# One causal-mask and row-maximum scheme, two routing strands and shared weight memory in a two-layer attention and expert kernel

## Chip, cores and metric

The kernel runs on one core of a Trainium2 chip. The metric is the device time of one execution in microseconds (us), and the figure for a kernel is the median of its runs. A profile is one more execution, recorded by the hardware; it has a time of its own.

A core has five instruction streams: PE (matrix products; the profile shows its weight loads apart, as PEld), DVE (vector work and row reductions), ACT (activations, exponentials), POOL (general work, and the indirect DMAs here) and SP (issues DMAs). Each engine takes its instructions in the order in which they were built. PE's results land in PSUM, which has eight banks of 128 partitions by 512 fp32 columns; DVE and ACT read them from there.

## The reference

`x` is [2, 2048, 256] in fp32. Cut to what matters:

```python
xn = layernorm(x)
s  = linear_attention(xn)        # rope, elu(q)+1, elu(k)+1, sum_k k v, / denominator, @ W_out
g  = silu(block(xn))             # see below
x  = x + s * g

xn = layernorm(x)
s  = attention(xn)               # Wq, Wk, Wv: 16 heads of 2*16 columns, causal softmax, Wo
g  = silu(xn @ int4_grid(kernel) + bias + (xn @ a) @ b)
x  = x + s * g

def block(x):                    # 16 heads of 16
    q, k, v = rope(ln1(x) @ Wqkv)
    x = x + causal_softmax(q k^T / 4) v @ Wproj
    flat = ln2(x)                                    # 4096 tokens
    gates = softmax(flat @ Wgate);  top 2 of 8 experts
    place = running count of the expert's tokens;  kept if place < 1024
    y_e = gelu(slots_e @ W1[e] + b1[e]) @ W2[e] + b2[e]
    return x + sum over the two experts of gate * y_e[place]
```

## The kernel before

`x` stays in SBUF as `xr`, 32 tiles of 128 tokens. Three stages follow one another.

**Layer-0 attention, with the linear attention beside it.** There are 8 groups of 4 heads (2 batches × 4). In a group, queries and keys lie turned in `qt` and `kt`, [128, 2048] each, one head in each 32 rows, so that four heads' products run in the four row groups of PE. A *unit* of the loop in `run_attention` (L514) holds two passes.

- Pass A (`pass_a`, L528): for 128 queries (tile t) and up to 512 keys (block k), each of 4 heads computes scores on PE into a bank of its own (L536), and DVE takes the largest of each row. Where the block holds the diagonal (k == t // 4) DVE does this with `tensor_tensor_reduce` (L543), which adds the causal constants of `causal`, a [128, 512] slice of the constants, and leaves the maximum; elsewhere with `tensor_reduce` (L547). The maxima are subtracted from the queries afterwards (`subtract`).
- Pass B (`pass_b`, L555 on): the same scores transposed (L562). Where they hold the diagonal, `hide` (L500) adds the mask on PE, by four bf16 products of an identity and a mask, each in 32 rows (L505). ACT takes exponentials out of the banks (L574). Later products with v (L804 in layer 0, L1557 in layer 1) sum over keys.

In a unit, the heads run in two halves, i = 0 and 2: pass A for heads i and i+1, pass B for the other two, in the order A(i), B(i+2), A(i+1), B(i+3), then pass B's masks, then the exponentials. There are 40 units in a group, with 640 pairs of heads in pass A in each layer: 256 of these pairs hold the diagonal.

Beside them run the preparation of the next group (`normalise0`, `norm`, `project`: normalise, turn, project, rotate on POOL, turn into qt and kt), the linear attention (`lin_keys`, `lin_out`, ending in stores of `lo` to `s_dram`, L1166), and at the end of each group of tiles the residual (L866), the second layernorm (statistics at L476 and L478 on DVE and small POOL operations), the logits (L930) and the picks: maxima, running counts, places and ways back (L940 to L987, some 35 small DVE operations). Tokens go to their slots by indirect DMAs from POOL (L1000).

**Experts.** For 2 halves × 8 experts: SP loads W1 (L1319), W2 (L1321), b2 (L1323) and the tokens `xe` (L1326); PE turns the tokens (L1335), multiplies by W1 (L1341) and W2 (L1347); results are stored (L1352). W1 and W2 each have two buffers of the pool that opens after the attention's pool has closed. The first `xe` waits for all sends. The constants of layer 1 are loaded behind it.

**Layer-1 attention**, same two passes with 32-wide heads; it starts with the normalised tiles `hn` (L1442), turned tiles `xt`, loads of `wg` (L1458), projections (L1468, L1483), and the gathers of expert results (L1403) for the mix of the later tiles.

In both attention stages a planner decides the order. Each piece of work is a step with a strand (its kind: S the products of both passes, A the maxima, B the exponentials, prep, sub, V, end, lin, moe, send, mix, gate, pair), an engine, a cost, and what it reads and writes. Steps of one strand on one engine keep their order; between strands the planner searches (a beam over short stretches) for the order that does most work, and gives out memory, the eight PSUM banks (kind "s") among it. The order found is then emitted, engine by engine. `others` in both stages lists parts with the unit at which they become due.

Names that come up below: `cst` the constants, `ident_h` and `mask_h` identity and mask for `hide`, `vt` the values with ones beside them (filled by DVE at L658), `lt` the low-rank gate's input, `carried` new memory.

## Time and profile before

| | us |
|---|---|
| median of 3 runs (lowest, highest) | 3483.42 (3477.35, 3490.22) |
| the profiled execution, its own time | 3508.01 |
| its span | 3506.2 |
| mean granted PE clock in it | 0.97 |
| busy PE / weight loads / DVE / ACT / POOL | 3350.0 / 2373.5 / 2163.6 / 1682.6 / 1660.5 |

Stages of that execution, by the marks in its timeline:

| stretch (us) | what runs |
|---|---|
| 0 to 32 | loads, constants, first tiles up to the first product of pass A at 31.59 |
| 32 to 1430 | layer-0 attention, linear attention beside it |
| 1430 to 1505 | last residuals, layernorm, logits, picks, sends; the linear attention's last tiles; first expert loads |
| 1505 to 1985 | experts |
| 1985 to 2050 | first projections of layer 1, gathers |
| 2050 to 3506 | layer-1 attention |

Other groups of the profile that are used below, in the form line, operation, count, mean:

| line | engine | what | count | mean ns |
|---|---|---|---|---|
| L562 | PE | pass B products, 256 or 128 columns | 9216 | 388 |
| L574 | ACT | exponential | 2304 | 576 |
| L804 | PE | values, layer 0 | 4608 | 381 |
| L1341 | PE | first expert product, 512 columns | 512 | 600 |

How to read it. A line of a group gives line, engine, operation, output and inputs with the tile's name, partitions by elements, the count, the busy time and the mean of one instruction; behind the bar stands the idle time of the engine just before, and what ended it. A line of the timeline gives the start, the duration, the engine (SPq is SP's queue of DMA issues), the line, the operation, a count where equal ones follow one another, and in brackets the idle time before it and its releaser. Matmul durations overlap, since four row groups work at once, so a mean of 559 ns does not mean that one ends each 559 ns.

### The profile page before, as it was taken

How to read it: one execution, taken by the hardware profiler on the slowest of the kernel's cores; microseconds unless marked ns; L12 is line 12 of the kernel's file. 1: busy time of each engine (PE TensorE's matmuls, PEld its weight loads, DVE VectorE, ACT ScalarE, POOL GpSimd, SP SyncE). 2: the span in 40 equal slices, each digit the busy share in tenths (PEclk: the TensorE clock that was granted, in tenths of full speed). 3: DMA queues.
4: the chain of work that ended last, by engine and by line, in shares of the span. 5: the costliest groups of instructions: out<-in, count | busy, mean ns of one | idle time of the engine just before them, and what ended most of it. 6: DMA issues, size and time to landing. Idle time of an engine off the chain costs nothing.

```text
span 3506.2 us, 81341 instructions
## 1 busy us (share of the span) xinstructions
PE 3350.0 (96%) x33814; PEld 2373.5 (68%) x33814; DVE 2163.6 (62%) x5599; ACT 1682.6 (48%) x3336; POOL 1660.5 (47%) x2223
## 2 busy tenths in 40 slices
PE   6999999999999999689989999999999999999998
PEld 4767777776777776456666556666776767777775
DVE  4777777777777877421121266667766657666774
ACT  3565555554555554311111265555445554554554
POOL 4443222323332221400000167989876657877877
PEclk7999999999999999789999999999999999999999
DMA  5000000000000000143333221010001010000000
GB/s 181 2 2 2 8 8 8 20 16 26 10 10 5 14 14 12 38 156 113 114 100 113 76 67 45 23 51 29 24 11 36 14 42 17 15 17 21 11 26 25
DMA packets 99508, 133.24 MB, mean 38 GB/s; under 512 B 9395, under 2 KB 76671, under 8 KB 99138
## 3 DMA queue, kind: packets, MB, share of 16 engines
q1 hardware_dynamic: 92994, 114.14, 10.1%
q0 software_dynamic: 6144, 13.88, 1.3%
q8 instruction: 266, 4.36, 0.5%
q14 instruction: 104, 0.85, 0.1%
HBM read 93.15 MB, written 37.75 MB: 37 GB/s over the span
## 4 chain that ended last, share of the span: by engine, by line
PE 45%; POOL 7%; DVE 2%; ACT 1%; issue 1%; DMA 1%; POOLq 0%; ACTq 0%; DVEq 0%
PE s L562 7%; PE s L536 7%; PE s L1347 6%; PE s L1341 6%; PE s L1557 6%; PE s L1468 3%; PE s L1526 2%; POOL ps L1542 2%; PE s L1563 2%; POOL ps L1543 2%; PE s L1605 2%; PE s L1483 1%; POOL ps L1538 1%; PE s L505 1%; PE s L1642 1%
## 5 line engine op out<-in xcount | busy, mean ns | idle before, releaser
L574 ACT ACTIVATE pt<-s 128x512 f32<-128x512 f32 (+1 forms) x2304 | 1168.9, 576 | 713.6 <-PE s L562 249.0
L562 PE MATMUL s<-qt,kt 32*128 32x256 f32 (+1 forms) x9216 | 1292.6, 388 | 7.9 <-ACT pt L574 4.4
L536 PE MATMUL s<-kt,qt 32*128 32x512 f32 (+3 forms) x5120 | 1269.7, 559 | 10.2 <-ACT pt L574 2.3
L547 DVE TENSOR_REDUCE mx<-s 128x1 f32<-128x512 f32 x1536 | 961.5, 682 | 185.0 <-PE s L536 101.9
L562 PEld LDWEIGHTS s<-qt,kt 32*128 32x128 f32 x9216 | 984.6, 185 | 62.0 <-ACT pt L574 16.2
L536 PEld LDWEIGHTS s<-kt,qt 32*128 32x128 f32 x5120 | 530.0, 186 | 170.0 <-issue 94.2
L543 DVE CUSTOM_DVE_ANT_0 s<-s,cst 128x128 f32<-128x128 f32 (+3 forms) x1024 | 482.3, 513 | 120.0 <-PE s L536 82.9
L1538 POOL TENSOR_TENSOR ps<-pt 128x1024 f32<-128x1024 f32 (+1 forms) x160 | 344.5, 2153 | 144.7 <-ACT pt L574 118.5
L743 POOL TENSOR_TENSOR ra<-raw,rope 128x128 f32<-128x128 f32 x128 | 58.6, 458 | 671.0 <-ACT raw L755 604.7
L1542 POOL TENSOR_TENSOR ps<-ps,pt 128x1024 f32<-128x1024 f32 x128 | 303.7, 2373 | 85.9 <-ACT pt L574 80.8
L1526 PE MATMUL s<-mh,ones_h 3*128 3x512 bf16 (+1 forms) x1152 | 317.3, 367 | 0.7 <-ACT mh L1519 0.7
L804 PE MATMUL s<-pt,vt 128*32 128x256 f32 (+1 forms) x4608 | 280.7, 381 | 5.3 <-issue 4.6
L1543 POOL TENSOR_TENSOR ps<-ps,pt 128x1024 f32<-128x1024 f32 (+1 forms) x128 | 269.2, 2103 | 10.0
L1557 PE MATMUL s<-pt,vt 128*32 128x256 f32 (+1 forms) x4608 | 271.3, 374 | 0.5 <-ACT pt L574 0.3
L1350 DVE TENSOR_TENSOR ye<-s,b 128x256 f32<-128x256 f32 x64 | 27.2, 424 | 391.6 <-PE s L1347 391.6
L1342 ACT ACTIVATE hm<-s,b1c 128x512 f32<-128x512 f32 x128 | 87.9, 687 | 359.6 <-PE s L1341 359.6
L1347 PE MATMUL s<-w,hm 128*128 128x256 f32 x1024 | 226.4, 382 | 8.5 <-ACT hm L1342 8.5
L1341 PE MATMUL s<-xt,w 128*128 128x512 f32 x512 | 226.4, 600 | 8.3 <-DVE xt L1282 8.3
L804 PEld LDWEIGHTS s<-pt,vt 128*32 128x32 f32 x4608 | 136.7, 112 | 135.0 <-issue 31.7
L1557 PEld LDWEIGHTS s<-pt,vt 128*32 128x32 f32 x4608 | 134.3, 110 | 136.4 <-DVE mx L547 18.0
L1347 PEld LDWEIGHTS s<-w,hm 128*128 128x128 f32 x1024 | 196.2, 192 | 42.9 <-ACT hm L1342 8.9
L505 PE MATMUL s<-mask_h,ident_h 32*128 32x256 bf16 x2048 | 197.7, 270 | 1.6 <-issue 1.6
(267 smaller groups left out, 4086.0 us busy)
## 6 DMA issues: line engine op xcount, KB each, us to landing
w<-in_L_ffn_W_dram SPq DMA_DIRECT2D x32, 1024.0 KB, 6.2
gl<-g_dram SPq DMA_DIRECT2D x64, 256.0 KB, 3.0
slots_in<-zero SPq DMA_DIRECT2D x8, 1024.0 KB, 10.2
xe<-slots_in SPq DMA_DIRECT2D x16, 512.0 KB, 8.0
slots_out<-ye SPq DMA_DIRECT2D x16, 512.0 KB, 7.2
xr<-in_L_attn_x_dram SPq DMA_DIRECT2D x4, 1024.0 KB, 5.6
s_dram<-lo SPq DMA_DIRECT2D x16, 256.0 KB, 2.0
hn<-in_L_attn_x_dram SPq DMA_DIRECT2D x16, 256.0 KB, 2.7
```

The lines of the kernel that those rows point to most:

```text
L536: nc.tensor.matmul(s.t[:, :w], g.qt.t[r, t * P : (t + 1) * P], g.kt.t[r, 512 * k : 512 * k + w], start=True, stop=True)
L543: nc.vector.tensor_tensor_reduce(s.t[:, :w], s.t[:, :w], causal[:, 512 - w :], 1.0, -3e38, ALU.add, ALU.max, to)
L547: nc.vector.tensor_reduce(to, s.t[:, :w], AX.X, ALU.max)
L562: nc.tensor.matmul(s.t[:, at], g.kt.t[r, kj * P : (kj + 1) * P], g.qt.t[r, QC * c + q0 : QC * (c + 1)], start=n == 0, stop=n == 1 and not ...
L574: S("B", "ACT", t_act(w), lambda: nc.scalar.activation(pt.t[:, j, :w], s.t[:, :w], AF.Exp, scale=0.25), r=[s], w=[(pt, j)])
L804: nc.tensor.matmul(av.t[32 * j : 32 * j + 32, q0:QC], vts[G.vn][:, kj, j], pt.t[:, j, at], start=n == 0, stop=n == len(tiles) - 1,)
L1341: nc.tensor.matmul(ps, w1[:, k, f * P : (f + 1) * P], xt[:, k], start=k == 0, stop=k == 1)
L1347: nc.tensor.matmul(ps[:, :D], hm[:, f, s * P : (s + 1) * P], w2[:, f], start=f == 0, stop=f == FF // P - 1)
L1526: return lambda: nc.tensor.matmul(s.t[:, :w_], ones_h[r], G.mh[c].t[r, 512 - w_ :], start=False, stop=last)
L1538: nc.gpsimd.tensor_tensor(ps.t[:, :, q0:], pt.t[:, :, same], pt.t[:, :, odd], ALU.add)
L1542: nc.gpsimd.tensor_tensor(ps.t, ps.t, pt.t[:, :, even], ALU.add)
L1557: nc.tensor.matmul(av.t[32 * j : 32 * j + 32, q0:QC], G.vt.t[:, kj, j], pt.t[:, j, at], start=n == 0, stop=False)
```

## The change

Seven edits, in one diff.

1. *Bank pairs.* PSUM's eight banks become one tile, and a buffer may ask for an even and an odd bank together. Pass A of two heads writes the two halves of a pair, and one `tensor_reduce` over [128, 2, w] gives both maxima.
2. *Mask on PE in layer 0's pass A.* On the diagonal, `hide` now adds the mask `mask_q` to the last 128 columns of each head's scores, after both heads' products and before pass B's own masks: 2 × 4 bf16 products of 32 rows and 128 columns for a pair. Layer 1 keeps `tensor_tensor_reduce`, one for each head, with its causal tile in memory of its own; the constants shrink from 1052 to 668 columns. A third set of `rep` copies and products at the start makes `mask_q`.
3. *Two strands for the routes.* What was "moe" is split: "moe" keeps statistics, scaling, turning and logits, "pick" has the picks.
4. *Carried memory.* Four tiles [128, 2048] are kept for the whole kernel. They serve as the two `qt` and the two `kt` of both layers, and, in between, as the two buffers of W1 and the two of W2.
5. *Layer 1's first tiles.* `hn`, `wg` and `xt` of layer 1 move to the pool that is open while the experts run; there is one `lt` in place of two.
6. *Start.* Tokens are loaded in pieces of 2, 2, 12 and 16 tiles (before: 4 × 8); the first four tiles are normalised in two parts of two; the fills of `vt` move from DVE to POOL and cover the ones' half alone; the turning into qt and kt, which followed each second `project`, becomes `turned_round` and is emitted one round later.
7. *Due times.* Batch 1's linear parts: from unit 172 on, one in each 9, where it was 180 and 7.5.

Counted in the built streams of all instructions, before and after: PE 22478 and 26578, DVE 5601 and 4068, ACT 3338 and 3338, POOL 2230 and 2249.

```diff
-    def __init__(self, kind):
-        self.kind, self.n, self.uses, self.t = kind, None, 0, None
+    def __init__(self, kind, pair=False):
+        self.kind, self.pair, self.n, self.uses, self.t = kind, pair, None, 0, None
...
-                for i, x in enumerate(st.since[b.kind]):
+                for i in range(0, len(since), 2) if b.pair else range(len(since)):
+                    x = since[i]
+                    if b.pair and x is not None:
+                        x = max(x, since[i + 1]) if since[i + 1] is not None else None
...
+    carried = [keep.tile([P, T], F32, name=f"carried{n}") for n in range(4)]
+    held = {
+        kind: [lambda n=n: carried[n] for n in range(at, at + 2)] for kind, at in (("qt", 0), ("kt", 2))
+    }
...
-    load_x(0)
+    load_x(0, 2)
+    load_x(2, 4)
...
-    load_x(1)
+    load_x(4, 16)
...
-    load_x(2)
-    load_x(3)
+    load_x(16, 32)
...
-    for n, c in enumerate((C_ID, C_AFTER)):
+    for n, c in enumerate((C_ID, C_AFTER, C_CAUSAL)):
...
-    def banks(ps, names):
-        return [lambda n=n: ps.tile([P, 512], F32, tag=n, name=n, bufs=1) for n in names]
+    def banks(ps):
+        all_ = ps.tile([P, Plan.BANKS, 512], F32, name="banks")
+        return lambda i, pair: all_[:, i : i + 2] if pair else all_[:, i]
...
-    def hide(out, j):
+    def hide(out, j, mask):
         r = slice(32 * j, 32 * j + 32)
         for q in range(4):
-            nc.tensor.matmul(out, ident_h[r, q], mask_h[r, q].rearrange("p n k -> p (n k)"), start=False, stop=q == 3)
+            nc.tensor.matmul(out, ident_h[r, q], mask[r, q], start=False, stop=q == 3)
...
-        def pass_a(g, t, k, j, w, mx, parts):
-            s, r, out = Buf("s"), slice(32 * j, 32 * j + 32), (mx, t, k, j)
...
+        def pass_a(g, t, k, i, w, mx, parts):
+            s, out, diagonal = Buf("s", True), (mx, t, k, i), k == t // 4
...
+            def products(x):
+                return S("S", "PE", t_row(w), lambda: score(x), r=[(g.qt, t), *((g.kt, n) for n in keys)], w=[(s, x)], on=i + x)
+            def rest():
+                for x in range(2) if diagonal and causal is None else ():
+                    S("S", "PE", T_HIDE / 2, lambda x=x: hide(s.t[:, x, w - P : w], i + x, mask_q), r=[(s, x)], w=[(s, x)], on=i + x)
+                if diagonal and causal is not None:
+                    for x in range(2):
+                        S("A", "DVE", t_dve(w) + 0.19, lambda x=x: nc.vector.tensor_tensor_reduce(
+                            s.t[:, x, :w], s.t[:, x, :w], causal[:, 512 - w :], 1.0, -3e38, ALU.add, ALU.max,
+                            mx.t[:, t % 2, i + x, k : k + 1],
+                        ), r=[(s, x)], w=[(*out, x)])
+                        parts.append((*out, x))
+                    return
+                S("A", "DVE", t_dve(2 * w), lambda: nc.vector.tensor_reduce(
+                    mx.t[:, t % 2, i : i + 2, k], s.t[:, :, :w], AX.X, ALU.max
+                ), r=[(s, 0), (s, 1)], w=[out])
+                parts.append(out)
...
+                if a:
+                    products, after_a = pass_a(g, t, k, i, wa, mx, parts)
                 for x in range(2):
                     if a:
-                        plan.pace = pass_a(g, t, k, i + x, wa, mx, parts)
+                        plan.pace = products(x)
...
+                if a:
+                    after_a()
                 for rest, _ in more:
                     rest()
...
-        for vt in vts:
-            nc.vector.memset(vt, 1.0)
+        for vt in vts:
+            nc.gpsimd.memset(vt[:, :, :, 16:], 1.0)
...
-            S("moe", "DVE", 0.35, less_top, r=[lg], w=["gates"])
+            S("pick", "DVE", 0.35, less_top, r=[lg], w=["gates"])
...
-            S("moe", "DVE", 1.2, ways_back, r=["places"], w=["places"])
+            S("pick", "DVE", 1.2, ways_back, r=["places"], w=["places"])
...
-                    if G.b == 0 and t % 4 == 0:
+                    if G.b == 0 and t == 0:
+                        parts.append(lambda: normalise0(0, 2))
+                        parts.append(lambda: normalise0(2, 2))
+                    elif G.b == 0 and t % 4 == 0:
                         parts.append(lambda t=t: normalise0(t))
                     parts.append(lambda t=t: norm(G, t))
+                if t:
+                    parts.append(lambda t=t - 2: turned_round(G, t))
                 for n in range(2):
                     parts.append(lambda t=t + n: project(G, t))
+            parts.append(lambda: turned_round(G, NT - 2))
...
-            start, every = ((0, 7.5), (180, 7.5))[b]
+            start, every = ((0, 7.5), (172, 9.0))[b]
...
-                w1 = wk.tile([P, 2, FF], F32, name="w1")
+                w1, w2 = carried[e % 2].rearrange("p (k f) -> p k f", k=2), carried[2 + e % 2].rearrange("p (f n) -> p f n", n=D)
                 nc.sync.dma_start(w1, w1_in[e])
-                w2 = wk.tile([P, FF // P, D], F32, name="w2")
                 nc.sync.dma_start(w2, w2_in[e])
...
-                qt=slots(wk, "qt", 2, [P, T]), kt=slots(wk, "kt", 2, [P, T]), vt=slots(wk, "vt", 2, [P, NT, 4, 32]),
+                **held, vt=slots(wk, "vt", 2, [P, NT, 4, 32]),
...
-                hn=slots(wk, "hn", 1, [P, 2, D]), wg=slots(wk, "wg", 1, [P, 3, 2, P]),
-                xt=slots(wk, "xt", 1, [P, 2, T]), m=slots(wk, "m", 2, [P, 2, 4]),
+                hn=slots(w, "hn", 1, [P, 2, D]), wg=slots(w, "wg", 1, [P, 3, 2, P]),
+                xt=slots(w, "xt", 1, [P, 2, T]), m=slots(wk, "m", 2, [P, 2, 4]),
```

## The prediction

> **What bounds the kernel now.** I read the page's first part and its 40 slices, then busy time by stage, then the timeline at the two stage borders, then the groups of the attention.
>
> ```profile
> PE 3350.0 (96%) x33814; PEld 2373.5 (68%) x33814; DVE 2163.6 (62%) x5599; ACT 1682.6 (48%) x3336; POOL 1660.5 (47%) x2223
> PEclk7999999999999999789999999999999999999999
> ```
> ```profile
> 32.00:150.00 118.00, 106.79 (x990) 73.95 (x987) 84.34 (x238) 57.93 (x131) 51.78 (x147) 0.91 0.13 46
> 150.00:1430.00 1280.00, 1262.22 (x14050) 930.78 (x14052) 952.03 (x2679) 723.49 (x1521) 398.04 (x964) 0.98 0.04 11
> 1430.00:1505.00 75.00, 32.55 (x166) 24.64 (x158) 31.92 (x168) 14.08 (x29) 27.23 (x46) 0.65 0.29 98
> 2050.00:3506.00 1456.00, 1419.55 (x16572) 997.37 (x16570) 981.85 (x2260) 752.69 (x1453) 1128.05 (x953) 0.99 0.09 26
> ```
> The columns of the second view are the window, its length, busy time with count of PE, weight loads, DVE, ACT and POOL, granted clock, DMA share, GB/s. PE is busy 96% of the span, but in 1430 to 1505, between layer 0's attention and the experts, it works 32.6 of 75 us. In the two attention stages it is booked 98%; that is no proof that it streams all the time, since four row groups overlap and a matmul that waits for a bank is hidden under another's record.
>
> ```profile
> 1441.89 0.68 DVE L866 TENSOR_TENSOR xr<-xr,s 128x512 f32<-128x512 f32 x1
> 1446.14 0.75 DVE L476 BATCH_NORM_STATS2 ln_st<-xr 128x6 f32<-128x256 f32 x2
> ...
> 1456.88 0.17 DVE L940 TENSOR_REDUCE top<-s 128x2 f32<-128x16 f32 x1 [9.78 <-PE s L930]
> ```
> ```profile
> 1482.76 1.09 POOL L1000 DMA_INDIRECT slots_in<-x,to  x1 [5.55 <-issue]
> ```
> ```profile
> 1489.24 0.38 SPq L1319 DMA_DIRECT2D w<-in_L_ffn_W_dram  x1
> ...
> 1490.81 0.54 SPq L1326 DMA_DIRECT2D xe<-slots_in  x1
> ```
> ```profile
> 1502.03 1.30 PE L1335 MATMUL t<-cst,xe 128*128 128x128 f32 x5 [21.70 <-DMA w<-in_L_ffn_W_dram]
> ```
> The last tiles' residual (L866) is done at 1442.6. Their statistics start only at 1464.47, behind the picks of the tiles before them on DVE (those end at 1464.4; the two statistics and the two picks stand in one queue). From there to the last sends, their landing, the expert loads and the first expert matmul is one chain of 37.6 us. The transposes of L1335 wait 21.7 us.
>
> ```profile
> L536 PE MATMUL s<-kt,qt 32*128 32x512 f32 (+3 forms) x5120 | 1269.7, 559 | 10.2 <-ACT pt L574 2.3
> L547 DVE TENSOR_REDUCE mx<-s 128x1 f32<-128x512 f32 x1536 | 961.5, 682 | 185.0 <-PE s L536 101.9
> L543 DVE CUSTOM_DVE_ANT_0 s<-s,cst 128x128 f32<-128x128 f32 (+3 forms) x1024 | 482.3, 513 | 120.0 <-PE s L536 82.9
> L505 PE MATMUL s<-mask_h,ident_h 32*128 32x256 bf16 x2048 | 197.7, 270 | 1.6 <-issue 1.6
> ```
> These are pass A's products, its two kinds of row maximum, and the mask matmuls that exist now for pass B alone. I fitted the length of 266 uninterrupted row-group stretches of layer 0 to the matmuls in them: 163, 194, 152 and 177 ns for an L536 of 128, 256, 384 and 512 columns (each within some 22 ns), and 6 with an error of 22 for one of L505. A product of 128 columns costs as much as one of 512, so these stretches are set not by streaming but by how fast DVE and ACT give the eight banks back: a unit needs four maxima, spaced 0.61 to 0.65 us, and four exponentials of 0.58 to 0.60.
>
> **The change, part by part**, against the execution's own 3508.0 us (span 3506.2 and 1.8 around it). The median of the runs, 3483.4, is 0.993 of that; the last step scales by it.
>
> *Start, −1.* The two ones-fills of vt (2 × 1.76 us on DVE, until 14.1, right where the first statistics begin) go to POOL with half the elements, as 2 × 0.98 by the row of a POOL memset of 512. DVE and PE get a third mask: one cast of 0.69 and four matmuls of 0.23. The statistics, over two tiles (0.67 for 1.34), can start some 3 us earlier. Against that, a second POOL chain for tiles 2 and 3, 15.80 to 21.92 now for four tiles and bound by its small operations, comes ahead of the first rotation, and two start loads more stand in SP's queue. Ends −4 and +2; the two nearly cancel, so −1.
>
> *Border to the experts, −29.* With two strands the middle tiles' statistics (at 1446.14, their residual done at 1425) needn't queue behind the picks before them (1437.07 to 1446.05), nor the last ones' behind the middle's. Their logits are then there by about 1436 and, 10.7 us after 1442.6 (the 1464.47 to 1475.2 of now), by 1453.3; the picks run one behind another, 1446 to 1453.6 and 1453.6 to 1460.9 (7.5 and 7.3 us as now), and the last sends begin 22 us sooner. The linear strand's operations on DVE, PE and ACT (up to 1473) fall between; I leave it 2. In the new order the first two experts' weights go into the qt/kt slots that the last two groups free, so ahead of the expert's inputs only b2 is issued. From the landed sends (1489.24) to the first matmul it is 12.8 us now; one landing of 512 KB alone I estimate at 4, half of page row xe's 8.0, which shares the queues with 2 MB of weights: −8.8. Together −29. What is queued behind: the first weight load waits on SP for the last reads of group 6, and the linear strand's stores and loads stand behind it; its last store is issued at 1473.36, which is after the sends' new time. If that store leads, 22 shrinks to 9.4 (1482.76 − 1473.36), and with most of the loads' gain under it the end is −15; the other is −33 (no 2 for the strand, landing in 2).
>
> *Border to layer 1, −4.* Its normalised tiles, weights and transposes get memory of their own, so the first two pairs of tiles and wg are ready while the experts run. Now L1468 begins at 1992.86, the last expert matmul ends at 1984.1; I take it to 1988.4, since the transposes (1.4 us each, L360) remain. The gathers of L1403, at 1988.27, wait for the last outputs' landing and don't move. Ends 0 and −6.
>
> *Causal mask of layer 0's pass A on PE, +12.* 8 groups × 16 query tiles × 4 heads × 4 = 2048 more bf16 matmuls of 128 columns, and as many weight loads: 2048 × 6 ns from the fit = 12. The other end is the rows' serial price: eight such loads take 0.44 us in a row (one group of eight L505 loads at 1000.16), times 256 head pairs = +113. The lower end is 0. I take the fit: it is the row of this very operation in these stretches, with cover from waits for banks. That cover is the 53 us in which weight loads between 150 and 1300 were released by DVE, and 52 by ACT; it shrinks with the next step.
>
> *Maxima in pairs, −20.* One instruction stands for two in 640 pairs of layer 0 and 384 of layer 1. Spacing of a maximum fits 0.08 + 1.08 ns a column, so a pair of plain ones saves 0.075 us (384 pairs, 29 us); a diagonal pair also loses its slower read-out (spacing 0.51 for 384 columns where a plain one would be 0.47, and 0.65 for 0.61 at 512): 0.145 (256 pairs, 37 us). In layer 1, plain pairs only: 29. DVE sheds 95 us in all. Of this only what DVE paces shows: its released waits, 53 in layer 0, are 53/1150 of the time, but DVE and ACT alternate as pacers, and ACT's four exponentials stay at 2.3 us a unit. Ends 0 and −45; I take a fifth of the 95, −20.
>
> *Mode switches, +10.* The built PE stream changes between row, column and full tiles 31 times more in layer 0 and 59 in layer 1. A switch shows 0.31 us (issue in front of L804: 20.3 us in 66 times): 90 × 0.31 = 28 at most, 0 if they fall into waits; a third.
>
> *Rigid pairs, +4.* A pass-A pair needs an even and an odd bank free together, and both are held until one longer maximum (1.2 us by the fit) ends. Products waited for L547 34 times in 150 to 1300, 11.9 us; if each in both layers grows by 0.3 us, half a maximum, it is 68 × 0.3 = 20; as the banks' work is no more than before, I take 4. Ends 0 and 20.
>
> *The rest, 0:* turned rounds one later, the linear parts of batch 1 re-timed, one lt buffer for two. They hide under 98% PE booking; without that cover lt costs 8 gate parts × 0.60 us (a product of 512 columns, L1341), 5.
>
> Sum: −1 −29 −4 +12 −20 +10 +4 = −28; 3480, times 0.993 = **3455**.
>
> **A rule against the change.** The row above says 6 ns for a mask matmul. The Trainium skill, "TensorE: Matmul & The Clock Gate", on the back-to-back issue gap, gives about 81 ns for each matmul of 128 columns in a stream of weight load and matmul. An estimate by that page: 2048 × 81 ns = 166 us, and the sum would be slower by about 126 us. The trace's pair rows (0.55 us for eight of 256 columns, in two row groups) already stay under it.
>
> **Rivals.**
> *Slower: PE in order pays for the masks.* Place: diagonal units of layer 0. The eight loads stand in PE's one queue ahead of pass B's masks, and the maximum can't start before them. For it: PE is booked 98%, 0.44 us of loads in one stretch; against it the 6 ns. It decides above (28 + 12)/256 = 0.16 us a pair. Midway from there to 0.44 is 0.30: +77 for the +12, 3545, scaled 3520; at 0.44 it is 3556.
> *Same: the linear tail or SP's queue takes the border's gain.* For it: the store at 1473.36 and PE's linear matmuls up to 1472.5 lie after the new send time; against: they don't feed the experts. Then −8 for the −29 and 0 for the −4: −3 in all, 3480 scaled.
> *Larger gain: banks pace the stretches throughout.* Relief −45 instead of −20: −53, 3431 scaled. For it: the flat fit; against: ACT's equal share of the waits.
> *It doesn't do what it says:* in the built streams the first weight load is at place 45 of SP, DVE falls from 5601 to 4068 instructions and PE grows from 22478 to 26578, so this is out, save that the scheduler's placing of the last statistics is a plan and not a time.
>
> **How the numbers follow.** Forecast 0.40 (its own range 3440 to 3470), larger gain 0.20, same 0.18, slower 0.22. A measurement of this kernel tells about 0.5%, 17 us: faster is under 3466, slower over 3501. Faster: 0.20 + nearly nine tenths of 0.40, 0.56; slower 0.22 and a rest, 0.23; same 0.21. Range 3405 to 3520: the low end is the larger gain with the border's −33 and no price for switches and pairs (−53 −4 −10 −4 −2 = −73, 3411), a little further for the start; the high end is the slower rival's middle, which leaves half of it out.
>
> **What would show it.** Right: L1335's wait falls from 21.7 us to under 10, and from L866's last residual to the first L1335 it is some 30 us, not 59.5; the stage of layer-0 attention is no longer than its 1398 us (32 to 1430), with maxima of two heads near 1.2 us, and DVE's busy time is down by some 95 us; L1468 starts within 5 us of the last L1347. Wrong: mask rows with a fit near 100 ns, waits for PE in front of the paired maximum that are longer than the relief, the last send still near its distance of 40 us from L866, or layer 1, which gets no masks, growing by over 20 us: then pairs and switches were priced too low.

## The result, and the profile after

The changed kernel takes 3462.65 us (median of 6 runs, 3459.48 to 3466.86); the kernel before, beside it, 3488.22 (3477.35 to 3494.25). The ratio is 0.9936, with a 95% interval of 0.9922 to 0.9951: about 22 us less, or 25.6 by the medians, where the prediction said 28. The total came out as forecast. Its terms did not, and the experiments are mostly about that. The whole gain is also smaller than what another order of the same work moves (E8 below).

The profiled execution of the changed kernel took 3459.48 us. The one of the kernel before had taken 3508.01, some 20 us over its own median, so the comparison here is with a second profile of it (E1 below, 3487.26 us, span 3485.5). The views of both that follow are busy time by stage, each with the stage borders of its own timeline: layer-0 attention up to the end of its last product with v; from there to the first transposes of expert tokens (called the border here); experts and the turn to layer 1; and layer-1 attention from its first projection. Columns: window, length, busy time and count of PE, weight loads, DVE, ACT, POOL, granted PE clock, DMA share, GB/s. First the kernel before:

```profile
31.60:1398.50 1366.90, 1345.25 (x15058) 993.60 (x15058) 1033.81 (x2916) 780.74 (x1651) 450.76 (x1109) 0.99 0.05 15
1398.50:1474.80 76.30, 34.02 (x131) 26.50 (x131) 29.12 (x158) 14.36 (x29) 27.75 (x48) 0.59 0.26 82
1474.80:1963.90 489.10, 467.10 (x1673) 309.25 (x1673) 71.27 (x141) 96.19 (x139) 14.10 (x20) 0.98 0.33 106
1963.90:3485.50 1521.60, 1474.44 (x16920) 1029.70 (x16920) 1016.86 (x2360) 784.76 (x1508) 1159.18 (x1005) 0.98 0.09 29
```

and the changed kernel:

```profile
33.80:1412.20 1378.40, 1357.85 (x17140) 997.26 (x17139) 974.66 (x1804) 783.42 (x1663) 460.84 (x1126) 0.99 0.05 17
1412.20:1455.90 43.70, 21.57 (x91) 16.42 (x87) 21.23 (x98) 6.94 (x14) 18.59 (x32) 0.66 0.34 110
1455.90:1938.50 482.60, 464.98 (x1672) 308.81 (x1672) 73.59 (x152) 95.98 (x138) 10.76 (x17) 0.98 0.33 103
1938.50:3457.70 1519.20, 1470.78 (x16920) 1000.84 (x16920) 1006.09 (x1976) 784.49 (x1508) 1161.59 (x1008) 0.98 0.10 30
```

The whole gain is at the two borders: 76.3 to 43.7, and 489.1 to 482.6. Layer 0's attention became 11.5 us longer (5.3 in E9, a second profile of the changed kernel) and starts 2.2 later, and layer 1's is 2.4 shorter: with 75 us less of DVE work in all, the attention as a whole gained nothing.

The last routes and the first expert transposes in the timeline of the changed kernel:

```profile
1420.59 0.68 DVE L900 TENSOR_TENSOR xr<-xr,banks 128x512 f32<-128x512 f32 x1
1421.31 0.75 DVE L491 BATCH_NORM_STATS2 ln_st<-xr 128x6 f32<-128x256 f32 x2
...
1431.97 0.15 DVE L974 TENSOR_REDUCE top<-banks 128x2 f32<-128x16 f32 x1
```
```profile
1444.68 0.97 POOL L1034 DMA_INDIRECT slots_in<-x,to  x1 [0.30 <-issue]
```
```profile
1409.17 0.37 SPq L1359 DMA_DIRECT2D carried<-in_L_ffn_W_dram  x1
...
1450.24 0.43 SPq L1365 DMA_DIRECT2D xe<-slots_in  x1
```
```profile
1455.87 1.94 PE L1374 MATMUL t<-cst,xe 128*128 128x128 f32 x8 [11.85 <-DMA b<-in_L_ffn_b_dram]
```

In E1's timeline, the kernel before, the last statistics stood behind the picks:

```profile
1414.04 0.68 DVE L866 TENSOR_TENSOR xr<-xr,s 128x512 f32<-128x512 f32 x1
...
1436.51 0.16 DVE L987 TENSOR_TENSOR m<-m,room 128x4 f32<-128x4 f32 x1
1436.59 0.74 DVE L476 BATCH_NORM_STATS2 ln_st<-xr 128x6 f32<-128x256 f32 x2
```

There they start 21.9 us after the residual's end; now they follow it at once, and logits come 10.7 us later, as the prediction counted. The second expert's weights are loaded 41 us before the first tokens, and PE waits 11.9 us where it waited 21.7 (22.0 in E1). From the issue of the first token load to the transposes it is 5.6 us (11.5 in E1's timeline: 1463.29 to 1474.8).

The groups of the row maxima and of pass A's masks in the changed kernel:

```profile
L573 DVE TENSOR_REDUCE mx<-banks 128x2 f32<-128x1024 f32 (+3 forms) x1024 | 1121.2, 1122 | 348.6 <-PE banks L587 146.5
L567 DVE CUSTOM_DVE_ANT_0 banks<-banks,causal 128x384 f32<-128x384 f32 (+3 forms) x512 | 242.4, 514 | 55.1 <-PE banks L554 41.4
L520 PEld LDWEIGHTS <-ident_h 32*128 32x128 bf16 x4096 | 201.1, 93 | 30.2 <-issue 15.1
```
```profile
DVE mx L573 <- PE banks L587: 114.3, 153, 2.4
DVE mx L573 <- PE banks L520: 43.5, 55, 2.6
```

A maximum over two heads is one instruction of 1.12 us in the mean. The second view (waits of DVE between 150 and 1300: sum, times, longest) shows what took the place of the old waits: the paired maximum (L573) stands behind pass B's products (114 us), which are issued between the two heads', and behind the masks (43.5). The same view of E1 had

```profile
DVE mx L547 <- PE s L562: 59.8, 85, 3.4
DVE s L543 <- PE s L536: 37.2, 55, 2.2
DVE mx L547 <- PE s L536: 23.6, 39, 1.6
```

### The profile page after: what moved, and what is told of

Same layout as the page of the kernel before. It is cut to its first block, busy times and chain, and to the rows that moved or that the text cites. A ratio compares the mean times of both kernels' runs of the same rounds, so it can differ in the third digit from the quotient of the medians.

```text
span 3457.7 us, 84287 instructions
## 1 busy us (share of the span) xinstructions
PE 3329.6 (96%) x35870; PEld 2335.4 (68%) x35870; DVE 2085.8 (60%) x4066; ACT 1677.2 (49%) x3336; POOL 1667.9 (48%) x2242
## 4 chain that ended last, share of the span: by engine, by line
PE 79%; POOL 10%; DVE 4%; issue 3%; ACT 2%; DMA 1%; SPq 0%; POOLq 0%; DVEq 0%; ACTq 0%
PE banks L554 15%; PE banks L587 13%; PE banks L838 7%; PE s L1386 6%; PE s L1380 6%; PE banks L1599 6%; PE banks L520 4%; PE banks L1510 3%; PE banks L768 3%; POOL ps L1584 2%; POOL ps L1585 2%; PE banks L1568 2%; DVE mx L573 2%; PE banks L1100 2%; PE banks L1605 2%
## 5 line engine op out<-in xcount | busy, mean ns | idle before, releaser
L599 ACT ACTIVATE pt<-banks 128x512 f32<-128x512 f32 (+1 forms) x2304 | 1164.2, 575 | 713.5 <-PE banks L1568 209.7
L573 DVE TENSOR_REDUCE mx<-banks 128x2 f32<-128x1024 f32 (+3 forms) x1024 | 1121.2, 1122 | 348.6 <-PE banks L587 146.5
L554 PE MATMUL banks<-carried,carried 32*128 32x512 f32 (+3 forms) x5120 | 1244.5, 561 | 13.4 <-DVE mx L573 6.2
L587 PE MATMUL banks<-carried,carried 32*128 32x256 f32 (+1 forms) x9216 | 1243.0, 389 | 7.0 <-DVE mx L573 5.8
L587 PEld LDWEIGHTS banks<-carried,carried 32*128 32x128 f32 x9216 | 930.1, 186 | 43.8 <-DVE mx L573 9.4
L554 PEld LDWEIGHTS banks<-carried,carried 32*128 32x128 f32 x5120 | 488.2, 185 | 206.8 <-issue 111.3
L775 POOL TENSOR_TENSOR ra<-raw,rope 128x128 f32<-128x128 f32 x128 | 60.1, 469 | 558.0 <-ACT raw L787 480.4
L1568 PE MATMUL banks<-mh,ones_h 3*128 3x512 bf16 (+1 forms) x1152 | 298.4, 370 | 0.1
L567 DVE CUSTOM_DVE_ANT_0 banks<-banks,causal 128x384 f32<-128x384 f32 (+3 forms) x512 | 242.4, 514 | 55.1 <-PE banks L554 41.4
L1599 PE MATMUL banks<-pt,vt 128*32 128x256 f32 (+1 forms) x4608 | 274.0, 376 | 0.7 <-ACT pt L599 0.5
L838 PE MATMUL banks<-pt,vt 128*32 128x256 f32 (+1 forms) x4608 | 268.9, 371 | 1.9 <-DVE mx L573 1.4
L1386 PE MATMUL s<-carried,hm 128*128 128x256 f32 x1024 | 226.0, 382 | 8.0 <-ACT hm L1381 8.0
L1599 PEld LDWEIGHTS banks<-pt,vt 128*32 128x32 f32 x4608 | 135.1, 111 | 140.0 <-ACT pt L599 36.8
L838 PEld LDWEIGHTS banks<-pt,vt 128*32 128x32 f32 x4608 | 133.6, 110 | 118.1 <-issue 16.4
## 6 DMA issues: line engine op xcount, KB each, us to landing
slots_in<-zero SPq DMA_DIRECT2D x8, 1024.0 KB, 10.6
```

The source lines that it names most:

```text
L554: nc.tensor.matmul(s.t[:, x, :w], g.qt.t[r, t * P : (t + 1) * P], g.kt.t[r, 512 * k : 512 * k + w], start=True, stop=not (diagonal and cau ...
L573: S("A", "DVE", t_dve(2 * w), lambda: nc.vector.tensor_reduce(mx.t[:, t % 2, i : i + 2, k], s.t[:, :, :w], AX.X, ALU.max), r=[(s, 0), (s, ...
L587: nc.tensor.matmul(s.t[:, at], g.kt.t[r, kj * P : (kj + 1) * P], g.qt.t[r, QC * c + q0 : QC * (c + 1)], start=n == 0, stop=n == 1 and not ...
L599: S("B", "ACT", t_act(w), lambda: nc.scalar.activation(pt.t[:, j, :w], s.t[:, :w], AF.Exp, scale=0.25), r=[s], w=[(pt, j)])
L838: nc.tensor.matmul(av.t[32 * j : 32 * j + 32, q0:QC], vts[G.vn][:, kj, j], pt.t[:, j, at], start=n == 0, stop=n == len(tiles) - 1,)
L1386: nc.tensor.matmul(ps[:, :D], hm[:, f, s * P : (s + 1) * P], w2[:, f], start=f == 0, stop=f == FF // P - 1)
```

## Experiments

Twelve kernels ran, in three batches of four, each batch on one chip. The kernel before took 3482.1 us on the first chip, 3514.1 on the second and 3485.7 on the third, so kernels are compared by their ratio to it, or with one another inside a batch. A ratio does not take the chip out wholly: E7, whose edit costs some 10 us, is 21 to 24 above the changed kernel by the ratios, and its layer-0 stage, in the same order, took 1415.6 us on chip 2 where the changed kernel's took 1378.4 and 1372.2 elsewhere.

| | kernel | median us | ratio (95%) |
|---|---|---|---|
| | changed kernel, first measurement | 3462.65 | 0.9936 (0.9922 to 0.9951) |
| E1 | before again, chip 1 | 3486.03 | 1.0006 (0.9995 to 1.0017) |
| E2 | head by head, chip 1 | 3468.63 | 0.9960 (0.9949 to 0.9972) |
| E3 | pairs, layer 0's masks on DVE, chip 1 | 3446.91 | 0.9896 (0.9880 to 0.9912) |
| E4 | masks twice, chip 1 | 3522.46 | 1.0116 (1.0102 to 1.0130) |
| E5 | one strand, chip 2 | 3500.14 | 0.9964 (0.9951 to 0.9977) |
| E6 | no masks in layer 0, chip 2 | 3492.34 | 0.9926 (0.9906 to 0.9946) |
| E7 | first weights wait, chip 2 | 3510.75 | 0.9996 (0.9985 to 1.0008) |
| E8 | another draw of the planner, chip 2 | 3543.74 | 1.0088 (1.0075 to 1.0101) |
| E9 | changed kernel again, chip 3 | 3459.29 | 0.9927 (0.9910 to 0.9943) |
| E10 | old times of the linear parts, chip 3 | 3448.29 | 0.9894 (0.9876 to 0.9911) |
| E11 | mask steps empty, chip 3 | 3421.57 | 0.9822 (0.9804 to 0.9840) |
| E12 | masks on DVE, new start, chip 3 | 3434.97 | 0.9854 (0.9833 to 0.9874) |

**E1, the kernel before again** (no edit).

> The kernel before once more, for a second profile. Theory: the 3506.2 us span of the first profile holds PE-clock dips that most executions lack (five recorded half-clock stretches of 41 us in all between 270 and 880, against none there in the changed kernel), so the layer-0 stage comes out 10 to 20 us shorter here (first product of pass A to the last residual 1390 to 1400 us, not 1410), while the border from last residual to first expert transpose stays at 59 to 60 us. Rival: the stage is 1410 us again and its 23 us over the changed kernel's 1387 are the work of pairs and masks. Ratio to the kernel before: 1.000 within 0.002.

From the first pass-A product to the last residual it is 1382.4 us, not the first profile's 1410.3, a larger step than expected; the border in that measure is 60.7. So the first profile's 23 us over the changed kernel in layer 0 do not measure the change: that execution had 51 us at half clock between 150 and 1400, this one 13.7.

**E2, head by head.**

```diff
-            s, out, diagonal = Buf("s", True), (mx, t, k, i), k == t // 4
+            bufs, diagonal = [Buf("s"), Buf("s")], k == t // 4
...
-run_attention(plan, Group0, ..., between=True)
+run_attention(plan, Group0, ..., between=True, causal=causal0)
```

> The changed kernel with pass A as it was in both layers: one bank and one maximum for each head, and the diagonal's causal constants added by DVE in layer 0 too (the constants are as wide as before and the third mask at the start is gone). Theory 1 (pairs and masks nearly cancel): within 8 us of the changed kernel, that is 0.991 to 0.996 of the kernel before. Theory 2 (prediction's step: relief 20, less masks 12, switches 10, pairs 4, net gain small but the relief is real): no more than 6 us faster than the changed kernel. Rival (the relief of DVE is the main gain): 15 to 30 us slower than the changed kernel, 0.998 to 1.002 of the kernel before.

6 us over the changed kernel by the first medians, 8 to 12 by the ratios: pairs and masks together are worth about that, near theory 1. The planner's input is another one here, so the order differs too.

**E3, pairs with layer 0's masks on DVE** (`causal=causal0` alone of the diff above).

> The changed kernel, but in layer 0 the diagonal's mask is added by DVE again, a tensor_tensor_reduce for each head of a bank pair, as layer 1 does it (2048 bf16 products and their loads fewer on PE, 256 paired maxima become 512 single ones). The prediction's terms: masks 12 us less, the diagonal pairs' relief (37 of 95 us of DVE work, by its fifth 8 us) lost: 4 us faster to 4 us slower than the changed kernel. Rival, PE pays serially: 0.30 to 0.44 us for each of 256 pairs come back, 77 to 113 us faster. Rival, DVE paces layer 0: 15 to 37 us slower.

It is faster than the changed kernel by 0.0031 to 0.0040 of the time, 11 to 14 us (15.7 by the first medians), and 21.7 us faster than E2. As measured, the pairs of plain blocks gain 22 us, and the step that moves the masks to PE gives half of it or more back. These kernels also differ in the planner's order, which by itself can move more than that (E8), so both figures are of one order each and are not shown to be the edits' own. Both theories with a large effect missed; the prediction's ±4 did too.

**E4, masks twice.**

```diff
-        for q in range(4):
-            nc.tensor.matmul(out, ident_h[r, q], mask[r, q], start=False, stop=q == 3)
+        for n in range(4 * times):
+            q = n % 4
+            nc.tensor.matmul(out, ident_h[r, q], mask[r, q], start=False, stop=n == 4 * times - 1)
...
```

> The changed kernel with each mask of layer 0's pass A added twice on PE (2048 bf16 products and weight loads more; the same order of everything else, and the same result, as twice a very negative number hides as well as once). It measures the marginal price of such a product. The prediction's fit, 6 ns each: 12 us slower than the changed kernel (0.997 of the kernel before). No price, hidden under waits for banks: 0 to 4 us. Serial loads (0.44 us a pair): 113 us slower (1.026).

59.8 us over the changed kernel: 29 ns for each further product (59.8 / 2048), five times the fit of 6, nearly a quarter of a microsecond for a pair. By the ratios it is 63 to 66 us. The order of all else is the changed kernel's.

**E11, mask steps empty.** The planner sees the same steps and gives the same order; they emit nothing. The causal mask is missing from layer 0's maximum, and the exponentials' scale is smaller.

```diff
-S("S", "PE", T_HIDE / 2, lambda x=x: hide(s.t[:, x, w - P : w], i + x, mask_q), ...)
+S("S", "PE", T_HIDE / 2, lambda: None, ...)
...
```

> The changed kernel with the mask steps of layer 0's pass A kept in the plan but empty, so that all else stands in the same order and 2048 products and their loads are missing (the causal mask of the maximum is left out; the exponentials' scale is 0.05 so that no sum vanishes). Theory 1, linear: 50 to 62 us faster than the changed kernel, as the second copy cost 57 to 60; then the diagonal pairs' relief of DVE is 35 to 45 us. Theory 2, the first copy is half hidden under waits for banks: 16 to 35 us faster, relief 0 to 20. The prediction's 12 us would need 8 to 16.

37.7 us faster than E9 on the same chip, between the two theories: the first 2048 products cost 18 ns each, the next 2048 cost 29. If the second copy shows the full price, a good third of the first was hidden, less than theory 2 had. With E3 the other half follows, as far as E3's other order allows: masks cost 38, the step's net is 11 to 16, so the lighter diagonal maxima gave back 22 to 27. The stage in E11's profile:

```profile
34.50:1371.80 1337.30, 1316.41 (x15092) 961.45 (x15091) 969.14 (x1802) 782.42 (x1663) 462.38 (x1126) 1.00 0.05 16
```

and E9's, the changed kernel on the same chip:

```profile
32.60:1404.80 1372.20, 1351.22 (x17140) 992.48 (x17139) 974.61 (x1808) 783.18 (x1663) 462.85 (x1126) 0.99 0.05 17
```

34.9 us less with 2048 matmuls less and DVE, ACT and POOL as busy as before: it is PE's stream that became shorter. Part of the difference is clock: E9's stage holds 17.1 us at half clock, E11's and E4's 6.8 each. With half of that taken off, an estimate from the stages of E9, E11 and E4 (1372.2, 1337.3 and 1435.0 us, E4 on another chip), the first copy costs 30 us (15 ns a product) and the second 68 (33 ns).

**E6, no masks in layer 0**, with the steps gone from the plan as well, so that the order is another one.

> The changed kernel without the mask products of layer 0's pass A: the paired maxima stay, but run over unmasked diagonals (the exponentials' scale is 0.05 in place of 0.25, so that no sum vanishes). This leaves out the causal mask of the maximum. With the kernel whose masks are on DVE (3446.9) it splits the two halves of that edit. Theory 1, the price is linear: as much faster than the changed kernel as adding the masks twice was slower, 55 to 62 us, 3401 to 3408 (0.977), so that the diagonal pairs' relief of DVE is worth some 40 us and not 8. Theory 2, the first 2048 products hide in part under waits for banks: 16 to 35 us faster, 3428 to 3447, relief 0 to 20.

Hardly faster than the changed kernel (0.9926), where E11 with the same work is at 0.9822. E6 ran on chip 2 and with another order in layer 0, so its total decides nothing; that is why E11 kept the order. Its stages say more. Beside E7 on the same chip its layer-0 stage is 26.3 us shorter (1389.3 for 1415.6), with about as much half clock (51.2 and 54.6 us), and its layer 1, whose order is that of E7, is 23.5 us longer (1545.1 for 1521.6), with 90.9 us at half clock for 43.6. So the masks' price shows in layer 0 here too, and layer 1's clock hides it in the total; the six runs lie between 3477.35 and 3498.95.

**E5, one strand** (`S("pick", ...)` is `S("moe", ...)` again).

> The changed kernel with the picks back in the strand of the statistics and logits (one queue for each engine, as before). Theory, the prediction's step: the last statistics queue behind the picks before them again, the distance from the last residual to the first expert transposes goes from 35 us back to 50 to 57, and the run is 15 to 22 us slower than the changed kernel (0.998 to 1.000 of the kernel before). Rival, the linear strand's tail or SP's queue decides the border: distance 35 to 42, 0 to 7 us slower (0.9936 to 0.9955).

The border's measure stays at 35.2 us from the last residual, and 43.0 from the last product with v:

```profile
1450.79 0.68 DVE L900 TENSOR_TENSOR xr<-xr,banks 128x512 f32<-128x512 f32 x1
1451.50 0.75 DVE L491 BATCH_NORM_STATS2 ln_st<-xr 128x6 f32<-128x256 f32 x2
```
```profile
1485.98 1.94 PE L1374 MATMUL t<-cst,xe 128*128 128x128 f32 x8 [12.51 <-DMA b<-in_L_ffn_b_dram]
```

The picks before it had ended at 1449.86, ahead of the last residual; nothing queues. The wait that the prediction pointed at is gone here too, but with one strand: the two strands are not what shortened the border. In time E5 is 10.6 us faster than E7, which is all that E7's loads cost (next), so the strands have no effect that shows, though E5's layer 0 has another order than E7's.

**E7, first weights wait** for the sends (a dependency on each send for the loads of experts 0 and 1).

> The changed kernel, but the loads of the first two experts' weights wait for all sends, as they did before (they stay in the shared memory). The prediction's step: 7 to 10 us slower than the changed kernel, with the first expert transposes 9 us later after the last send. Rival, the token load alone takes nearly as long to land, so nothing was gained there: 0 to 3 us.

Against E5 and E8 on the same chip the border is 46.8 us for 43.0 and 44.3, and the stretch from the first transposes to the start of the last expert product 484.9 for 477.4 and 477.7: 10 to 11 us, of which most shows after the first transposes. The token load takes 10.0 us from issue to PE beside the weights (1484.30 to 1494.28) and 5.6 without them. The step held in size, not in place: the prediction put all 8.8 us ahead of the first transposes, where 2.5 to 3.8 show.

**E10, old times of the linear parts** ((180, 7.5) for batch 1).

> The changed kernel with the linear attention's parts of batch 1 due as before (from unit 180 on, one each 7.5). One strand for the routes did not lengthen the border, so the border's gain is not from the picks' strand. Theory: the earlier and sparser linear parts let the routing of the last tiles keep up with the attention; with the old times the stretch from the last product with v to the first expert transposes goes from 44 us back to 60 to 76 and the run is 10 to 30 us slower than the changed kernel. Rival, the times do nothing (the planner orders all of it anyway): within 6 us of the changed kernel, stretch 42 to 48.

The opposite of the theory: 11.0 us faster than E9. The border is 35.6 us, not 43.6:

```profile
1406.90:1442.50 35.60, 10.77 (x57) 8.94 (x54) 15.19 (x88) 4.30 (x9) 12.05 (x25) 0.64 0.36 112
```

With the new times the last linear tiles fall into the border (their last store is issued at 1444.66, with the old ones at 1411.98), and the last picks share DVE with them. In the changed kernel's timeline at that place:

```profile
1426.03 1.27 POOL L1073 TENSOR_TENSOR la<-lk,rope 128x512 f32<-128x512 f32 x1 [0.95 <-ACT lk L1154]
1426.22 1.20 DVE L1005 TENSOR_TENSOR hots<-hots,took 128x16 f32<-128x16 f32 x2
...
1428.82 1.23 DVE L1010 TENSOR_TENSOR a__215<-a__215,room 128x4 f32<-128x4 f32 x1
```

DVE operations of 0.17 us (L1005 and L1010 a batch later: 0.17 each) take 1.1 to 1.2 while POOL rotates; the four that are slowed here (L1005, L1007, L1008, L1010) lose some 3 us together, so the rest of the border's 8 is not traced. The Trainium skill, "SBUF — State Buffer", under Terms, calls the port pair that DVE and POOL share a lock held for a whole instruction; these rows agree. Besides the border's 8 us, the profiles differ by +2.5 in layer 0 and −7.4 in layer 1, whose order is the same and whose half-clock time is 43.9 us for 65.0.

**E8, another draw** (`random.Random(1)` in the planner).

> The changed kernel with another start value of the planner's random trials: the same work, placed in another order. It shows how far the order alone moves the time, which bounds what may be read from kernels that differ in a step. Theory: within 5 us of the changed kernel (3457 to 3468), so that differences of 15 us and more stand for the edits. Rival: 10 us and more away, then the differences of this study hold the planner's luck too.

The rival, by far: 1.0088 against 0.9936 or 0.9927, 53 to 56 us by the ratios for another order of the same work, and 43.6 beside E5 on the same chip. This draw of the changed kernel is slower than the kernel before, though its border, 44.3 us, is as short as the other's. On chip 2, against E7 (same order as the changed kernel), layer 0 is 6.7 us longer and layer 1 37.3:

```profile
1980.80:3539.70 1558.90, 1502.98 (x16920) 1015.41 (x16920) 994.23 (x1976) 786.23 (x1508) 1160.81 (x1008) 0.96 0.09 29
```

The count of instructions and their busy time on DVE, ACT and POOL are those of the other kernels; the clock is 0.96. What moved is mostly the time at half clock (last section): in layer 1 it is 111.6 us for E7's 43.6, and all five runs of E8 have a mean clock of 0.963 to 0.967, E7's twelve 0.970 to 0.976.

**E12, masks on DVE, new start**: E3 with the first tiles' shrinking queued ahead of the second tiles' scaling on ACT.

```diff
                         parts.append(lambda: normalise0(0, 2))
+                        parts.append(lambda: norm(G, 0))
                         parts.append(lambda: normalise0(2, 2))
...
```

> The kernel with the masks of layer 0's pass A on DVE, paired elsewhere, and with the first two tiles' shrinking put ahead of the second two's normalising on ACT. Theory: the start's loss comes from ACT's queue, where the first tiles' hn stands behind the scaling of tiles 2 and 3; the first product of pass A comes at 29.5 to 31.5 us in place of 32.5 to 33.8, and the kernel is 14 to 22 us faster than the changed one (0.987 to 0.990 of the kernel before). Rival: the start's gain is lost to the second pair of tiles, or the gain of masks on DVE was the planner's luck: less than 10 us faster than the changed kernel.

24.3 us faster than E9 on the same chip, and 50.7 faster than the kernel before: the best version of the study. But not for the reason given. `hn` comes at 18.42 in place of 23.11, and the first product of pass A at 34.28, later than in E3 (32.5):

```profile
18.42 0.91 ACT L749 ACTIVATE hn<-xr,ln_n 128x256 f32<-128x256 f32 x2 [1.56 <-POOL ln_n L481]
```
```profile
27.44 0.20 POOL L481 TENSOR_TENSOR ln_n<-ln_n,ln_t 128x2 f32<-128x2 f32 x1
27.59 0.46 POOL L775 TENSOR_TENSOR ra<-raw,rope 128x128 f32<-128x128 f32 x1
```

PE has finished the first projections at 23.85, but ACT's copy of them (L787) starts at 26.02, behind the scaling of the second pair of tiles (L727, from 25.03); then the first rotation (L775) waits on POOL for that pair's small operations. The gain was lost to the second pair, as the rival said. Its 12 us over E3 go with a shorter border (39.9 for 45.8) and 5.9 us less in layer 1, whose order is the same; they are not explained further. E12 with the linear parts' old times was not tried.

## The prediction, point by point

**Total.** 3455 against 3488.22 × 0.9936 = 3466 by the ratio (3462.65 by the median). Right in sign and size, through terms that cancel, and by luck: the prediction had no term for the planner's order, and the same change under another draw (E8) is slower than the kernel before. Of the signs that the prediction named, the border's came near (34.6 us from the last residual's end, 30 forecast; PE's wait 11.9, under 10 forecast), and DVE shed 75 us, not 95.

**Start, −1.** Wrong: +2.2 and +1.0 (first products at 33.8 and, in E9, 32.6; 31.6 before). The statistics did start 4 us earlier (10.18 for 14.10); the step let that about cancel with the second POOL chain, and did not count ACT's queue at all, where `hn` stood behind the scaling of tiles 2 and 3 (its own input was ready at 19.3, and it started at 23.11).

**Border to the experts, −29.** The size was right (76.3 to 43.7 is −32.6, and 2 us more in the experts' stretch), the cause in the main wrong. The weights' part, −8.8, measured 10 to 11 (E7). The part put down to the two strands, −22, does not come from them (E5): the wait that it named, statistics behind picks, was there (21.9 us in E1) and went, but it stays away with one strand. The linear parts' new times, counted at nothing, take 8 us of the border back (E10). Some 25 us are thus traced to no single edit: with the weights late again (E7) the border and the stretch to the last expert product are 46.8 + 484.9 us, and 76.3 + 480.0 in E1. E2, E5, E7 and E10 each undo one thing, E8 has another draw, and all have borders of 36 to 47. So it is not the luck of one draw; which part of the change lets the routes come closer to the attention's end was not shown, and no run undid two parts together.

**Border to layer 1, −4.** Right: from 9.1 to 4.5 us between the start of the last expert product and the first projection; the gathers begin 4.6 us after the last expert product's end, where it was 4.1.

**Causal mask on PE, +12.** A step that failed in size: 38 (E11), and 60 for a second copy (E4). The fit of 6 ns came from pass B's masks and had an error of 22, so it did not rule out the 18 that pass A's masks cost; the step took its middle as the price. Why the fit came out so low no run shows. The decision point of the slower rival, 0.16 us a pair, was nearly reached: 37.7 us over 256 pairs is 0.147. The 81 ns per matmul of the page that the prediction cites (the Trainium skill, "TensorE: Matmul & The Clock Gate", Back-to-back issue gap) is not reached here, at 18 to 29.

**Maxima in pairs, −20.** Too small in layer 0, if E2 and E3 are taken in spite of their other orders: some 22 for plain pairs (E2 to E3, of which 17 in the stage), 22 to 27 for the diagonal ones, near the "larger gain" rival's −45. In layer 1, where 29 us of DVE time were to go, DVE's busy time fell by 10.8 and no gain shows: with half of the half-clock time taken off, an estimate, its length is 1491.3 before (E1), 1492.5 head by head (E2) and 1493.5 in the changed kernel. PE is 97% busy there, which fits a stage that DVE does not pace; that was not tested by itself.

**Mode switches, +10, and rigid pairs, +4**, were not measured apart; they lie in the net of E2 to E3.

So masks and maxima, +12 − 20 in the prediction, were about +38 − 47, the second with E3's reservation. Both were mis-sized by some 26, in opposite directions.

## What to carry to other kernels

An edit that moves work from one engine to another is two terms, and each should be measured by itself: here one run with the work doubled and one with it left out, in the same order, gave the price that a fit over stretches had missed by a factor of three. In a kernel whose order is planned, an edit that changes the plan's input is compared with a repeat under another draw before a difference of one per cent is believed. A stage border is read by its chain, but the cause is shown only by undoing the edit.

## What was not expected of the hardware

The clock records of the traces show PE either at full or at half clock, in stretches of 3.4 us or a multiple (the last of a profile ends with it). Layer 1's stage has one order in all kernels of the changed form but E2 and E8, so the half-clock time in it, and its length, can be compared (us):

```
                 half clock   stage
E7                  43.6      1521.6
E10                 43.9      1518.5
after               51.4      1519.2
E11                 52.5      1520.4
E4                  55.8      1520.1
E3                  62.0      1526.4
E9                  65.0      1525.9
E5                  66.7      1527.6
E12                 69.8      1520.5
E2                  76.7      1530.9
E6                  90.9      1545.1
E8                 111.6      1558.9
```

Between E7 and E8, 68 us more at half clock go with 37 us more of stage, and between E7 and E6, in one order, 47 with 23.5: about half of it, which is what a half clock takes from a busy PE. It does not explain all: E12's stage is some 14 us shorter than half of its half-clock time would make it, counted from E7's. The Trainium skill, "TensorE: Matmul & The Clock Gate", under What's actually happening, has the two clock states and a window of some 3.4 us of activity; the records agree. The same instructions in the same order had from 43.6 to 90.9 us of it in a stage that is 97% busy, so this stage alone can differ by over 20 us between two profiles with no edit behind it; what starts such a stretch no run shows.

Chips differ too: on chip 2 the kernel before is 0.9% slower than on chip 1, and the profiles there, like the first one of the kernel before, hold waits of ACT and DVE that nothing in the program ends. From the waits view of E7 (sum, times, longest):

```profile
DVE un L847 <- remote: 22.4, 3, 9.0
ACT pt L599 <- remote: 18.1, 6, 7.3
```

No profile from chips 1 and 3 has such a line.
